# Letting layer 1 of a graph-network kernel begin inside the last pair of layer 0

## The chip, the cores and the metric

The kernel runs on one NeuronCore of a Trainium2 chip. The metric is the device time of one execution in microseconds (us). Its five engines have queues of their own and run side by side: TensorE (PE, matrix products), VectorE (DVE), ScalarE (ACT), GpSimd (POOL) and SyncE (SP, which here only issues DMA transfers). Each works through its queue strictly in order, and waits for the others by semaphores. The kernel before took 2484.26 us, the median of three runs (2483.71 to 2485.73).

## The reference

Two layers act on a batch of 64 matrices x of 256 x 256 (32 pairs of two), with one shared 256 x 256 matrix adj. All is float32.

```
# layer 0
h = max(layernorm(x), 0);  G = adj * adj
h = relu(G (h W1)); h = relu(G (h W2)); x = x + G (h W3)     # W1 256x512, W2 512x1024, W3 1024x256
# layer 1
h = max(layernorm(x), 0)
deg = adj.sum(0) + adj.sum(1) - diag(adj)
L = diag(deg)^-1/2 (diag(deg) - adj) diag(deg)^-1/2
U = eigenvectors of L (eigh)
x = x + U (relu((U^T h) V1 + b1) V2 + b2)                     # V1 256x128, V2 128x256
```

Layer 1 needs U, all the eigenvectors of a 256 x 256 symmetric matrix. They don't depend on x, so layer 0 can run while they are computed.

## The kernel before

**Two programs share the engines.** `Eigen.vectors` computes U and its transpose (tiles `u` and `ut`): a tridiagonal form, small eigenproblems of 16, and four levels of merging. It is a long chain of small steps, most on DVE. The class `Layers` does everything with x, pair by pair. Layer 0 of pair q is a sequence of PE products (`first`, `second`, `third`, `fourth`, `last`), each bank of results moved out of PSUM by ACT. `last` adds the result to x on DVE and gives x1. `norm1` then normalizes x1 for layer 1: eight ACT sums (`junk`), small DVE steps on 128 x 4 (`nm`, `v`, `tmp`, `s`, `scale`, `shift`), four ACT passes that write `h`. `turn_rows` transposes `h` on PE, with two ACT copies back, and `for_layer1` multiplies it by V1 (`L_gnn_W` against `h`) into the tile `hw`. In the program's products each instruction appears in the trace as two weight loads and two matmul rows (a transpose as one).

For pairs 0 to 29, x1 and hw are spilled to DRAM; those of the last two pairs (`KEPT = 2`) stay in SBUF.

**The order of the work on PE and ACT is written out by a planner.** The class `Pace` keeps a clock for each engine and estimated durations. The eigenvector program issues through `pace.now`, whose `chain` places an instruction at the time at which its inputs are ready; before it, `run` issues instructions of layer 0's two streams (`products`, for PE, and `rows`, for loading and normalizing) that can start earlier. `pace.finish()` issues what is left of the streams. So PE multiplies for layer 0 in the gaps of the eigenvector chain. DVE, POOL and SP keep their program order in this part or are ordered by the framework's scheduler.

**The hand-over to layer 1.** The last instructions of `vectors` are two products that ACT copies into `u` and `ut`, and a product that adds up counters of missed convergence over the partitions; DVE turns it into an integer `flag`. Then `pace.finish()` issues the rest of layer 0. After that `Eigen.mend` (L1690, L1691) has every engine load `flag` into a register and branch: with a flag over zero, a slower eigensolver is run. It is zero here, and every engine jumps over that body (about 70 PE and 15,000 DVE instructions). The framework's DVE order puts one `x <- x, bank` addition of the last pair ahead of the branch, the other behind it; the rest of the last pair's normalization, its transposes and its product with V1 stand behind it too.

**Layer 1** (`layer1`) takes the pairs in the order 30, 31, 0, 1, ..., 29. In step i it fetches the pair three steps ahead (`fetch`: hw of 256 KB and x1 of 512 KB by SP, L1971 and L1973), does `to_vectors` of pair i (PE `hw` against `u`, DVE `z`, ACT `s`, POOL `xb` = x1 + U b2), `from_vectors` of pair i-1 (PE `s` against `ut`, ACT `g`) and `finish` of pair i-2 (PE `g` against V2, DVE `out`, a store by SP). Its tiles lie in memory that the eigenvector program's pools gave back, so the first transfer waits until every engine is past the branch.

Of the kernel before, what the change touches and what calls it, by code (L numbers as in the profile page):

```python
# [27 lines left out]
N = 256  # L28
P = 128
H = 2  # L30
PAIRS = 32
KEPT = 2
LN_EPS = 1e-5
EPS = 2.0**-24
BIG = 1.0e3
# [108 lines left out]
class Pace:  # L144
# [6 lines left out]
    LATER = {"PE": 0.2, "ACT": 0.1}  # L151

    def __init__(self, nc):
        self.slower = self.SLOWER
        self.now = Proxy(nc, self.chain)
        self.later = Proxy(nc, lambda op: op)
        self.clock = dict.fromkeys(ENGINES.values(), 0.0)
        self.written, self.read, self.streams, self.on = {}, {}, [], True
# [32 lines left out]
    def chain(self, op):  # L191
        if not self.on:
            return op.call(*op.args, **op.kwargs)
        late = self.LATER.get(op.engine, 0.0)
        self.run(self.ready(op) + late, "ACT" if op.engine == "ACT" else None)
        return self.issue(op, self.slower)

    def run(self, limit, whole=None):
# [14 lines left out]
    def complete(self, stream):  # L213
        while stream.more:
            if stream.head() is not None:
                self.issue(stream.op)
                stream.op = None

    def finish(self):
        self.run(float("inf"))  # L220
# [1474 lines left out]
class Layers:  # L1695


    def __init__(self, tc, ctx, ap, gt2, u, ut):
        self.tc, self.nc, self.ap = tc, tc.nc, ap
        self.gt2, self.u, self.ut = gt2, u, ut  # L1700
        pool = ctx.enter_context(tc.tile_pool(name="layers", bufs=1))
        self.kept = ctx.enter_context(tc.tile_pool(name="kept", bufs=KEPT))
        dram = ctx.enter_context(tc.tile_pool(name="dram", bufs=1, space=bass.MemoryType.DRAM))
        self.x1, self.hw = {}, {}
        self.x, self.h0, self.y1, self.y2, self.s2, self.p3, self.h1, self.new = ({} for _ in range(8))
        self.begun = set()
        self.spilled = {
            q: dram.tile([P, H * 2 * N], F32, name=f"x1_{q}") for q in range(PAIRS - KEPT)
        }
        self.spilled_hw = {  # L1710
            q: dram.tile([P, H * 2 * P], F32, name=f"hw_{q}") for q in range(PAIRS - KEPT)
        }
        self.w = {}
        for name in ("L0_gnn_W1", "L0_gnn_W2", "L0_gnn_W3", "L1_gnn_W1", "L1_gnn_W2"):
            rows, cols = ap[name].shape
            self.w[name] = pool.tile([P, rows // P, cols], F32, name=name)
        self.b1 = pool.tile([P, P], F32, name="b1")
        self.eye = pool.tile([P, P], F32, name="eye")
        self.b2 = pool.tile([P, N], F32, name="b2")
        self.u1 = pool.tile([P, H], F32, name="u1")  # L1720
        self.ub2 = pool.tile([P, H, N], F32, name="ub2")
# [11 lines left out]
        for h in range(H):  # L1733
            yield self.nc.sync.dma_start(out=x[:, h], in_=self.view(self.ap["x"], q)[:, h])

    def open(self, ctx, name, io, work, banks):

        self.io = ctx.enter_context(self.tc.tile_pool(name=name + "_io", bufs=io))
        self.wp = ctx.enter_context(self.tc.tile_pool(name=name + "_work", bufs=work))
        self.sp = ctx.enter_context(self.tc.tile_pool(name=name + "_stat", bufs=2))  # L1740
        self.ps = ctx.enter_context(self.tc.tile_pool(name=name + "_psum", bufs=banks, space=PSUM))

    def view(self, t, q):
        return t[2 * q : 2 * q + 2].rearrange("b (h p) f -> p h b f", p=P)
# [3 lines left out]

    def group(self, out, pairs):
        for i, (lhsT, rhs) in enumerate(pairs):  # L1750
            self.nc.tensor.matmul(out, lhsT=lhsT, rhs=rhs, start=i == 0, stop=i == len(pairs) - 1)  # L1751

    def products_of(self, out, pairs):
        for i, (lhsT, rhs) in enumerate(pairs):
# [51 lines left out]
    def products(self):  # L1806


        yield lambda: 0 in self.h0
        yield from self.first(0)  # L1810
        yield from self.second(0)
        for q in range(PAIRS):
            more = q + 1 < PAIRS
            yield from self.third(q)
            if q > 0:
                yield lambda: q - 1 in self.h1
                yield from self.turn_rows(q - 1)
            yield from self.fourth(q, 0)
            if q > 0:
                yield from self.for_layer1(q - 1)  # L1820
            if more:
                yield lambda: q + 1 in self.h0
                yield from self.first(q + 1)
            yield from self.fourth(q, 1)
            if more:
                yield from self.second(q + 1)
            yield from self.last(q)
        yield lambda: PAIRS - 1 in self.h1
        yield from self.turn_rows(PAIRS - 1)
        yield from self.for_layer1(PAIRS - 1)  # L1830

# [127 lines left out]

    def turn(self):  # L1960

        nc = self.nc
        nc.vector.tensor_reduce(self.u1, self.u, AX.X, OP.add)  # L1963
        for h in range(H):
            nc.vector.tensor_scalar(self.ub2[:, h, :], self.b2, self.u1[:, h : h + 1], None, OP.mult)

    def fetch(self, q):
        x1, hw = self.x1.get(q), self.hw.get(q)
        if x1 is None:
            hw = self.io.tile([P, H, 2, P], F32, tag="hw", name="hw1")  # L1970
            self.nc.sync.dma_start(out=hw.rearrange("p h b k -> p (h b k)"), in_=self.spilled_hw[q])  # L1971
            x1 = self.io.tile([P, H, 2, N], F32, tag="x", name="x1")
            self.nc.sync.dma_start(out=x1.rearrange("p h b f -> p (h b f)"), in_=self.spilled[q])  # L1973
        return x1, hw

    def to_vectors(self, x1, hw):

        nc = self.nc
        z = self.wp.tile([P, H, 2, P], F32, tag="z", name="z")
        ps = self.bank()  # L1980
        for m in range(H):
            self.group(
                ps[:, m * N : (m + 1) * N],
                [
                    (self.u[:, h, m * P : (m + 1) * P], hw[:, h].rearrange("p b k -> p (b k)"))
                    for h in range(H)
                ],
            )
        nc.vector.tensor_tensor(
            z.rearrange("p h b k -> p (h b) k"),  # L1990
            ps.rearrange("p (g k) -> p g k", k=P),
            self.b1.unsqueeze(1).to_broadcast([P, H * 2, P]),
            OP.add,
        )
        s = self.wp.tile([P, H, 2, P], F32, tag="s", name="s")
        nc.scalar.activation(s, z, AF.Relu)
        xb = self.wp.tile([P, H, 2, N], F32, tag="xb", name="xb")
        for b in range(2):
            nc.gpsimd.tensor_tensor(xb[:, :, b, :], x1[:, :, b, :], self.ub2, OP.add)  # L1999
        return s, xb  # L2000

    def from_vectors(self, s):

        g = self.wp.tile([P, 2 * N], F32, tag="g", name="g")
        ps = self.bank()
        for b in range(2):
            self.group(
                ps[:, b * N : (b + 1) * N], [(s[:, m, b, :], self.ut[:, m, :]) for m in range(H)]
            )
        self.nc.scalar.copy(g, ps)  # L2010
        return g

    def finish(self, q, g, xb):
        nc = self.nc
        out = self.io.tile([P, H, 2, N], F32, tag="out", name="out")
        for m in range(H):
            ps = self.bank()
            for b in range(2):
                at = b * N + m * P
                self.group(  # L2020
# [2 lines left out]
            nc.vector.tensor_tensor(flat(out)[:, m, :], flat(xb)[:, m, :], ps, OP.add)  # L2023
            nc.sync.dma_start(out=self.view(self.ap["out"], q)[:, m], in_=out[:, m])

    def layer1(self):

        ahead = 3
        order = [*self.x1, *self.spilled]
        got = {i: self.fetch(order[i]) for i in range(KEPT + ahead)}  # L2030
        mid, tail = {}, {}
        with self.tc.manual_schedule():
            for i in range(PAIRS + 2):
                if KEPT + ahead <= i + ahead < PAIRS:
                    got[i + ahead] = self.fetch(order[i + ahead])
                if i < PAIRS:
                    mid[i] = self.to_vectors(*got.pop(i))
                if 0 <= i - 1 < PAIRS:
                    s, xb = mid.pop(i - 1)
                    tail[i - 1] = self.from_vectors(s), xb  # L2040
                if 0 <= i - 2:
                    self.finish(order[i - 2], *tail.pop(i - 2))
# [7 lines left out]
def tile_kernel(ctx: ExitStack, tc: tile.TileContext, ap):  # L2050
    pool = ctx.enter_context(tc.tile_pool(name="shared", bufs=1))
    gt2, u, ut = (pool.tile([P, H, N], F32, name=c) for c in ("gt2", "u", "ut"))
    layers = Layers(tc, ctx, ap, gt2, u, ut)
    with ExitStack() as inner:
        pace = Pace(tc.nc)
        eigen = Eigen(tc, inner, ap, gt2, pace)
        layers.open(inner, "l0", io=2, work=1, banks=4)

        layers.nc = pace.later
        for op in layers.load(0):  # L2060
# [2 lines left out]
        layers.load_weights()  # L2063
        eigen.load_rest()

        layers.nc = pace.later
        pace.streams = layers.streams()
        with tc.manual_schedule(engines={mybir.EngineType.PE, mybir.EngineType.Activation}):
            eigen.vectors(u, ut)
            pace.finish()  # L2070
        layers.nc = tc.nc
        eigen.mend(u, ut)
    layers.open(ctx, "l1", io=5, work=4, banks=8)
    layers.turn()
    layers.layer1()


INS = [
# [30 lines left out]
```

## Time and profile before

| | |
|---|---|
| median of the runs | 2484.26 us |
| the profiled execution | 2484.25 us, span on the core 2482.4 us |
| PE busy | 2401.1 us, 97% |
| DVE, ACT, POOL busy | 2152.8, 1009.6, 474.2 us |
| mean granted TensorE clock | 0.993 |
| DMA | 90.03 MB; mean share of the engines 0.75 to 0.80 in layer 1 |
| `flag` written | 2265.24 us into the span |
| first transfer of layer 1 | 2288.97 us |
| last matmul | 2477.9 us |

All positions in time below are microseconds from the start of the span. A row of the timeline gives the start and length of a run of like instructions, the engine, the line, the operation, the tiles as out<-in with shapes, the number of rows, and in brackets the idle time ahead of it and the engine and tile that ended it. Line 189 is the helper through which the planner issues everything; line 1751 is the helper of layer 1's products. PE is pipelined, so the length of a run includes the drain of its last matmul; from the start of one run to the start of the next is the better measure. In a row with windows of time, the figures behind the engines are the granted TensorE clock as a share of full speed, the DMA share, and GB/s.

### The profile page before, as it was taken

To read this page: it belongs to the slowest core of one execution; us is meant where nothing else is said; L and a number is where in the kernel's file an instruction comes from. 1 tells how busy PE (TensorE), PEld (TensorE's weight loads), DVE (VectorE), ACT (ScalarE), POOL (GpSimd) and SP (SyncE) were. 2 spreads that over 40 slices of the span, in tenths; PEclk is the share of its full clock that TensorE was granted. 3 is DMA by queue.
4 is the path that set the end of the run, shared out by engine and by line. 5 is a ranking of instruction groups with operands and counts; after the bars stand their busy time and mean duration, and the time that the engine had idled before them with its cause. 6 is when DMAs were issued, how large, how long until landed. Compare 5 with 4: busy or idle time off the path is not lost. (4 is left out here: it accounts for less than half of the span.)

```text
span 2482.4 us, 38245 instructions
## 1 busy us (share of the span) xinstructions
PE 2401.1 (97%) x8986; PEld 1551.4 (62%) x8986; DVE 2152.8 (87%) x13409; ACT 1009.6 (41%) x2826; POOL 474.2 (19%) x1625
## 2 busy tenths in 40 slices
PE   7999999999999999999999999999999999998899
PEld 4666655666565566656556666665566666665788
DVE  7999999999999999999999889998888887973333
ACT  4334444434444433344444244443444434343222
POOL 2333333334333111111110000000000000000343
PEclk9999999999999999999999999999999999999899
DMA  3000000000000000000000000000000000001476
GB/s 111 18 13 15 22 22 19 22 22 5 22 22 18 22 22 22 5 22 22 22 18 30 10 22 22 22 22 22 18 22 26 22 22 22 6 21 34 166 252 203
DMA packets 59401, 90.03 MB, mean 36 GB/s; under 512 B 5792, under 2 KB 42784, under 8 KB 59168
## 3 DMA queue, kind: packets, MB, share of 16 engines
q1 hardware_dynamic: 59168, 87.52, 10.7%
q8 instruction: 73, 1.20, 0.2%
q14 instruction: 160, 1.31, 0.2%
HBM read 47.13 MB, written 40.37 MB: 35 GB/s over the span
## 5 line engine op out<-in xcount | busy, mean ns | idle before, releaser
L189 PE MATMUL bank<-y,L_gnn_W 128*128 128x512 f32 x2048 | 905.5, 593 | 1.3 <-ACT y L189 1.3
L189 PEld LDWEIGHTS bank<-y,L_gnn_W 128*128 128x128 f32 x2048 | 379.3, 190 | 427.2 <-issue 410.9
L189 PE MATMUL bank<-L_gnn_W,s 128*128 128x256 f32 x2048 | 464.7, 381 | 2.2 <-ACT s L189 2.2
L189 PEld LDWEIGHTS bank<-L_gnn_W,s 128*128 128x128 f32 x2048 | 384.3, 191 | 51.8 <-ACT s L189 2.6
L189 ACT ACTIVATE s<-bank 128x512 f32<-128x512 f32 x384 | 224.3, 586 | 179.5 <-PE bank L189 178.2
L189 PE MATMUL bank<-gt,s 128*128 128x256 f32 x1024 | 230.3, 379 | 1.7 <-ACT s L189 1.7
L189 PE MATMUL bank<-L_gnn_W,y 128*128 128x512 f32 x512 | 228.8, 592 | 0.0
L189 PEld LDWEIGHTS bank<-gt,s 128*128 128x128 f32 x1024 | 192.1, 190 | 36.1 <-issue 9.6
L1999 POOL TENSOR_TENSOR xb<-x,ub 128x512 f32<-128x512 f32 x64 | 79.6, 1267 | 601.4 <-ACT junk L189 506.3
L189 ACT ACTIVATE s<-nn,guard 128x1 f32<-128x1 f32 x254 | 74.3, 293 | 252.2 <-DVE nn L189 235.7
L189 POOL COPY m<-xr 128x1 f32<-128x1 f32 x254 | 55.6, 219 | 548.1 <-DVE xr L189 535.7
L189 ACT ACTIVATE h<-x,shift,scale 128x256 f32<-128x256 f32 x256 | 135.9, 590 | 59.3 <-DVE shift L189 59.1
L189 ACT COPY y<-bank 128x512 f32<-128x512 f32 x192 | 110.8, 580 | 115.8 <-PE bank L189 114.8
L189 PEld LDWEIGHTS bank<-L_gnn_W,y 128*128 128x128 f32 x512 | 95.3, 190 | 97.8 <-issue 90.6
L189 ACT ACTIVATE junk<-xr 128x254 f32<-128x254 f32 (+63 forms) x127 | 45.9, 361 | 263.8 <-DVE xr L189 263.4
L189 ACT ACTIVATE junk<-x,nm 128x256 f32<-128x256 f32 x256 | 129.0, 504 | 26.8 <-DVE nm L189 22.2
L189 ACT ACTIVATE junk<-x 128x256 f32<-128x256 f32 x256 | 105.5, 412 | 83.1 <-DVE x L189 68.8
L189 DVE SCALAR_TENSOR_TENSOR A<-xr,wc,A 128x255 f32<-128x255 f32 (+63 forms) x381 | 139.3, 367 | 0.0
L189 DVE SCALAR_TENSOR_TENSOR A<-wr,q,A 128x255 f32<-128x255 f32 (+63 forms) x381 | 138.6, 365 | 0.0
L189 PEld LDWEIGHTS psB<-ident,ac 128*128 128x128 f32 x381 | 44.8, 135 | 148.1 <-PE bank L189 76.6
L189 DVE SCALAR_TENSOR_TENSOR q<-q 128x1 f32<-128x1 f32 (+1 forms) x576 | 119.4, 208 | 16.4 <-ACT q L189 5.6
L189 PE MATMUL bank<-gt,h 128*128 128x256 f32 x512 | 120.5, 386 | 0.4 <-ACT h L189 0.4
(604 smaller groups left out, 4375.4 us busy)
## 6 DMA issues: line engine op xcount, KB each, us to landing
x<-x SPq DMA_DIRECT2D x60, 512.0 KB, 3.6
x<-in_x_dram SPq DMA_DIRECT2D x64, 256.0 KB, 3.7
out_dram<-out SPq DMA_DIRECT2D x64, 256.0 KB, 2.2
hw<-hw SPq DMA_DIRECT2D x60, 256.0 KB, 2.6
L_gnn_W<-in_L_gnn_W_dram SPq DMA_DIRECT2D x1, 2048.0 KB, 11.0
L_gnn_W<-in_L_gnn_W_dram SPq DMA_DIRECT2D x1, 1024.0 KB, 13.6
L_gnn_W<-in_L_gnn_W_dram SPq DMA_DIRECT2D x1, 512.0 KB, 6.4
mask<-in_c_blk_dram SPq DMA_DIRECT2D x2, 256.0 KB, 2.6
```

Source lines behind the costliest of these rows:

```text
L189: return op.call(*op.args, **op.kwargs)
L1999: nc.gpsimd.tensor_tensor(xb[:, :, b, :], x1[:, :, b, :], self.ub2, OP.add)
```

## The change

- The planner's streams are no longer emptied ahead of the branch. Behind the flag product, 6 us of PE work by the planner's clock (`FLAG_US`) are issued (`pace.go_on`), then the branch on all engines.
- Layer 1 is now issued through the planner (`pace.now`, with `no_haste`: an instruction of layer 1 is placed one step behind its engine's clock, and stream instructions that are ready go in front). So products of layer 1 alternate with what is left of layer 0's last pair on PE.
- Layer 1's order becomes 0 to 10, 30, 31, 11 to 29. The stream's last part (transposes of pair 31 and its product with V1) is held back by `self.due` until step 8, then issued whole.
- `turn` (DVE: row sums of U and U b2) becomes the first thing behind the branch, in layer 1's written order.
- Layer 1 has pools of its own (`open1`) while layer 0's stay open: five buffers for fetched tiles, three instead of five for `out`, four for its work tiles, and PSUM banks taken in turn from a new pool of four and layer 0's pool of four (before: one pool of eight).

The PE queue of the changed kernel, as its built program has it (x counts program instructions): nine of the sixteen products of `fourth(31, 0)`, the flag's load and the branch, one more of them, then

```
hw(0),u x4 in turn with fourth(31,0) x6 | hw(1),u x4 in turn with for_layer1(30) x8
ut,s(0) x4 and hw(2),u x4 and ut,s(1) x4 in turn with fourth(31,1) x16
last(31) x4 in turn with V2,g(0) x4
hw(3) x4, ut,s(2) x4, V2,g(1) x4, ... five such steps, up to hw(7), ut,s(6), V2,g(5)
transposes of h(31) x8, for_layer1(31) x8, then hw(8) x4 ... to the end as before
```

Behind the branch, SP first issues hw and x1 of pairs 0, 1, 2, 3, 4, then of 5 as pair 0's are freed. DVE's order there is: `turn`, z(0), z(1), z(2), x(31) first half, out(0) first half, x(31) second half, out(0) second half, nm, z(3), out(1) first half, v, out(1) second half, tmp, tmp, s, s, scale, shift, z(4), out(2), ... ACT's is: s(0), p(31), s(1), hw(30), g(0), s(2), p(31), g(1), six of the eight sums of pair 31, s(3), a sum, g(2), a sum, the root, two of four `h`, s(4), `h`, g(3), `h`, s(5), g(4), ...

```diff
@@ -30,6 +30,8 @@
 H = 2
 PAIRS = 32
 KEPT = 2
+LAST_AT = 12
+FLAG_US = 6.0
 LN_EPS = 1e-5
 EPS = 2.0**-24
 BIG = 1.0e3
...
@@ -191,8 +193,10 @@
     def chain(self, op):
         if not self.on:
             return op.call(*op.args, **op.kwargs)
-        late = self.LATER.get(op.engine, 0.0)
-        self.run(self.ready(op) + late, "ACT" if op.engine == "ACT" else None)
+        due = self.ready(op) + self.LATER.get(op.engine, 0.0)
+        if self.no_haste:
+            due = max(due, self.clock[op.engine] + 0.01)
+        self.run(due, "ACT" if op.engine == "ACT" and not self.no_haste else None)
         return self.issue(op, self.slower)
 
     def run(self, limit, whole=None):
@@ -215,6 +219,9 @@
             if stream.head() is not None:
                 self.issue(stream.op)
                 stream.op = None
+
+    def go_on(self, us):
+        self.run(self.clock["PE"] + us)
 
     def finish(self):
         self.run(float("inf"))
...
@@ -1733,12 +1741,25 @@
         for h in range(H):
             yield self.nc.sync.dma_start(out=x[:, h], in_=self.view(self.ap["x"], q)[:, h])
 
-    def open(self, ctx, name, io, work, banks):
-
-        self.io = ctx.enter_context(self.tc.tile_pool(name=name + "_io", bufs=io))
-        self.wp = ctx.enter_context(self.tc.tile_pool(name=name + "_work", bufs=work))
-        self.sp = ctx.enter_context(self.tc.tile_pool(name=name + "_stat", bufs=2))
-        self.ps = ctx.enter_context(self.tc.tile_pool(name=name + "_psum", bufs=banks, space=PSUM))
+    def open(self, ctx):
+
+        self.io = ctx.enter_context(self.tc.tile_pool(name="l0_io", bufs=2))
+        self.wp = ctx.enter_context(self.tc.tile_pool(name="l0_work", bufs=1))
+        self.sp = ctx.enter_context(self.tc.tile_pool(name="l0_stat", bufs=2))
+        self.ps = ctx.enter_context(self.tc.tile_pool(name="l0_psum", bufs=4, space=PSUM))
+
+    def open1(self, ctx):
+
+        self.io1 = ctx.enter_context(self.tc.tile_pool(name="l1_io", bufs=5))
+        self.op = ctx.enter_context(self.tc.tile_pool(name="l1_out", bufs=3))
+        self.wp1 = ctx.enter_context(self.tc.tile_pool(name="l1_work", bufs=4))
+        self.ps1 = ctx.enter_context(self.tc.tile_pool(name="l1_psum", bufs=4, space=PSUM))
+        self.turns = 0
+
+    def bank1(self):
+
+        self.turns += 1
+        return (self.ps1 if self.turns % 2 else self.ps).tile([P, 512], F32, tag="bank", name="bank")
 
     def view(self, t, q):
         return t[2 * q : 2 * q + 2].rearrange("b (h p) f -> p h b f", p=P)
...
@@ -1825,7 +1846,7 @@
             if more:
                 yield from self.second(q + 1)
             yield from self.last(q)
-        yield lambda: PAIRS - 1 in self.h1
+        yield lambda: PAIRS - 1 in self.h1 and self.due
         yield from self.turn_rows(PAIRS - 1)
         yield from self.for_layer1(PAIRS - 1)
 
...
@@ -1967,17 +1988,17 @@
     def fetch(self, q):
         x1, hw = self.x1.get(q), self.hw.get(q)
         if x1 is None:
-            hw = self.io.tile([P, H, 2, P], F32, tag="hw", name="hw1")
-            self.nc.sync.dma_start(out=hw.rearrange("p h b k -> p (h b k)"), in_=self.spilled_hw[q])
-            x1 = self.io.tile([P, H, 2, N], F32, tag="x", name="x1")
-            self.nc.sync.dma_start(out=x1.rearrange("p h b f -> p (h b f)"), in_=self.spilled[q])
+            hw = self.io1.tile([P, H, 2, P], F32, tag="hw", name="hw1")
+            self.now.sync.dma_start(out=hw.rearrange("p h b k -> p (h b k)"), in_=self.spilled_hw[q])
+            x1 = self.io1.tile([P, H, 2, N], F32, tag="x", name="x1")
+            self.now.sync.dma_start(out=x1.rearrange("p h b f -> p (h b f)"), in_=self.spilled[q])
         return x1, hw
 
     def to_vectors(self, x1, hw):
 
-        nc = self.nc
-        z = self.wp.tile([P, H, 2, P], F32, tag="z", name="z")
-        ps = self.bank()
+        nc = self.now
+        z = self.wp1.tile([P, H, 2, P], F32, tag="z", name="z")
+        ps = self.bank1()
         for m in range(H):
             self.group(
                 ps[:, m * N : (m + 1) * N],
...
@@ -2023,15 +2044,21 @@
             nc.vector.tensor_tensor(flat(out)[:, m, :], flat(xb)[:, m, :], ps, OP.add)
             nc.sync.dma_start(out=self.view(self.ap["out"], q)[:, m], in_=out[:, m])
 
-    def layer1(self):
+    def layer1(self, pace):
+
 
         ahead = 3
-        order = [*self.x1, *self.spilled]
-        got = {i: self.fetch(order[i]) for i in range(KEPT + ahead)}
+        last = PAIRS - 1
+        order = [*range(LAST_AT - 1), last - 1, last, *range(LAST_AT - 1, last - 1)]
+        got = {i: self.fetch(order[i]) for i in range(ahead)}
         mid, tail = {}, {}
         with self.tc.manual_schedule():
+            self.turn()
             for i in range(PAIRS + 2):
-                if KEPT + ahead <= i + ahead < PAIRS:
+                if i == LAST_AT - 1 - ahead:
+                    self.due = True
+                    pace.finish()
+                if i + ahead < PAIRS:
                     got[i + ahead] = self.fetch(order[i + ahead])
                 if i < PAIRS:
                     mid[i] = self.to_vectors(*got.pop(i))
@@ -2051,10 +2078,10 @@
     pool = ctx.enter_context(tc.tile_pool(name="shared", bufs=1))
     gt2, u, ut = (pool.tile([P, H, N], F32, name=c) for c in ("gt2", "u", "ut"))
     layers = Layers(tc, ctx, ap, gt2, u, ut)
+    layers.open(ctx)
+    pace = Pace(tc.nc)
     with ExitStack() as inner:
-        pace = Pace(tc.nc)
         eigen = Eigen(tc, inner, ap, gt2, pace)
-        layers.open(inner, "l0", io=2, work=1, banks=4)
 
         layers.nc = pace.later
         for op in layers.load(0):
@@ -2063,16 +2090,16 @@
         layers.load_weights()
         eigen.load_rest()
 
-        layers.nc = pace.later
+        layers.nc, layers.now = pace.later, pace.now
         pace.streams = layers.streams()
         with tc.manual_schedule(engines={mybir.EngineType.PE, mybir.EngineType.Activation}):
             eigen.vectors(u, ut)
-            pace.finish()
-        layers.nc = tc.nc
+            pace.go_on(FLAG_US)
+        pace.on = False
         eigen.mend(u, ut)
-    layers.open(ctx, "l1", io=5, work=4, banks=8)
-    layers.turn()
-    layers.layer1()
+    pace.on, pace.no_haste, pace.slower = True, True, 1.0
+    layers.open1(ctx)
+    layers.layer1(pace)
 
 
 INS = [
```

## The prediction

> **What bounds the kernel now.** First the page's busy times and its 40 slices (62 us each).
>
> ```profile
> PE 2401.1 (97%) x8986; PEld 1551.4 (62%) x8986; DVE 2152.8 (87%) x13409; ACT 1009.6 (41%) x2826; POOL 474.2 (19%) x1625
> PE   7999999999999999999999999999999999998899
> PEclk9999999999999999999999999999999999999899
> ```
>
> TensorE bounds nearly everything. Only the first and the 37th and 38th slices fall below 9, and in the 38th the granted clock falls too. The change can therefore win only the hole around 2290 us. PE's own timeline shows that hole.
>
> ```profile
> 2283.42 3.25 PE L189 MATMUL bank<-p,gt 128*128 128x512 f32 x7
> 2301.48 0.47 PE L189 MATMUL bank<-eye,h 128*128 128x128 f32 x1 [14.80 <-ACT h L189]
> 2302.47 1.82 PE L189 MATMUL bank<-eye,h 128*128 128x128 f32 x7 [0.51 <-ACT h L189]
> 2304.80 3.85 PE L189 MATMUL bank<-L_gnn_W,h 128*128 128x128 f32 x16 [0.52 <-ACT h L189]
> 2309.32 6.24 PE L1751 MATMUL bank<-hw,u 128*128 128x256 f32 x16 [0.67 <-ACT hw L189]
> 2315.40 1.89 PE L1751 MATMUL bank<-ut,s 128*128 128x256 f32 x8
> ```
>
> PE ends pair 31's `last` at 2286.67, stands 14.80 us for that pair's `h`, and runs what follows at half speed: 16 rows of `hw,u` take 6.1 us to the next start, where eight like rows of `ut,s` later take 1.73 (2315.40 to 2317.13). What fills the hole is read from the chain that ended last.
>
> ```profile
> 2289.47 0.69 DVE x L189
> ...
> 2300.83 1.59 ACT h L189 x3
> ...
> 2309.32 168.56 PE bank L1751 x768
> ```
>
> It runs through pair 31's addition, normalization, transposes and V1 product, and from 2309.32 through products alone. From there the kernel is bound by PE at 5.18 us a pair, with DMA at 0.8. Last, what the branch costs: SP's waits around the hand-over, and the first row of DVE behind the branch.
>
> ```profile
> SPq L1971 <- PEq L1690: 17.9, 1, 17.9
> SPq L1971 <- ACTq L1690: 2.4, 1, 2.4
> SPq L1971 <- DVEq L1691: 2.0, 1, 2.0
> ```
>
> ```profile
> 2288.86 0.69 DVE L1963 TENSOR_REDUCE u<-u 128x2 f32<-128x512 f32 x1 [3.18 <-DVEq L1691]
> ```
>
> SP's first transfer (2288.97) waits for every engine: 17.9 us for PE, then 2.4 for ACT, 2.0 for DVE. Counted back, PE's load of the flag passed at 2288.97 - 2.0 - 2.4 = 2284.6, two microseconds ahead of PE's last matmul.
>
> **The change, step by step.** *What is removed: the hole.* From 2286.67 to 2315.40 are 28.73 us. The work in it at full speed is eight transposes 0.87 (pair 30's: 2266.52 to the next start 2267.39), the V1 product 1.79 (pair 30's: 2274.30 to 2276.09) and 16 rows of `hw,u` 3.46 (twice 1.73), in all 6.12. So 22.6 us are lost now. All this work stays, and so does the sum of the products: the same number for each pair, and layer 1 ends with the same steps. The order ahead of the branch is unchanged on PE, so both kernels agree up to there.
>
> *The branch inside PE's stream.* PE reaches it behind nine of `fourth(31, 0)`'s sixteen products: 2267.39 + 18 rows x 0.216 (32 rows take 2267.39 to 2274.30) = 2271.3. The flag is there at 2265.24, and ACT's last instruction ahead of its branch ends at 2268.55; PE is the last. How long PE stands, no row shows: before, it waited for `h` anyway. Above: DVE's 3.18 us. The Trainium skill speaks against the move too (Runtime: NRT & Kernel Launch, Instruction fetch mechanics): a taken branch to a target outside the fetched window stalls on a fetch. But it gives PE room for 2048 instructions, and PE's skipped body has some 70[...]. I take 1.0, nearer the low end, because PE's flag load passed two microseconds early, hidden behind queued products. The clean-up of layer 0's last additions, no longer ahead of DVE's branch, costs nothing: DVE then stands at the branch from 2265 on.
>
> *The first fetch.* Behind SP's wait are queued the ten transfers of pairs 0 to 4, and all later ones; PE's second product behind the branch waits for the first. Before, layer 1 began with pairs kept in SBUF and hid this. SP issues 0.1 after PE's passing, and hw lands 2.6 us later by the page's row:
>
> ```profile
> hw<-hw SPq DMA_DIRECT2D x60, 256.0 KB, 2.6
> ```
>
> So hw(0) is there at 2271.3 + 1.0 + 0.1 + 2.6 = 2275.0. One product of 0.43 lies in between: PE is idle 3.7 - 0.4 = 3.3 us. With branch 0.1 and landing 2.0 it is 1.8; with 3.2 and 3.0, 5.9. Pair 0's x1 is wanted by POOL only, whose `xb` is used some 25 us later. The second hw is behind 1 MB in the queue, wanted some 4 us after the first, with about 3 us to spare; `turn` (1.3 us of DVE) runs within PE's hole.
>
> *The clock.* Does a hole of 3.7 us with 0.4 us of work inside halve the clock? PE's timeline has two earlier gaps, and windows of half a microsecond show the clock around the second.
>
> ```profile
> 1720.33 1.91 PE L189 MATMUL bank<-L_gnn_W,s 128*128 128x256 f32 x4 [2.20 <-ACT s L189]
> ...
> 1786.46 1.24 PE L189 MATMUL psB<-ident,m 128*128 128x128 f32 x4 [3.47 <-DVE m L189]
> ```
>
> ```profile
> 1785.00:1785.50 0.50, 0.00 (x0) 0.00 (x0) 0.50 (x7) 0.00 (x0) 0.00 (x0) 0.90 0.00 0
> ...
> 1792.00:1792.50 0.50, 0.50 (x3) 0.33 (x3) 0.00 (x0) 0.00 (x0) 0.00 (x0) 0.78 0.00 0
> ```
>
> The clock (third figure from the end) fell at 1785.4, 2.4 us into an idle time of 3.47, and came back at 1792.2: 5.8 us of PE at half speed, 2.9 lost. At 2309.32 to about 2314.5 it was 5.1 us and 2.6. A gap of 2.20 (1720) did not lower it. The Trainium skill (TensorE: Matmul & The Clock Gate, Part 1) asks for a whole idle window of 3.4 us, counted by a free-running clock. By the page 0 here, since the product cuts the hole; by the row, which fell with a third of such a window busy, 2.7 in about half of the positions of the window. I follow the row: 1.3 (0 to 3.4).
>
> *Mixed products.* Products of both layers in turn cost no more than apart: each loads its own weights either way. ACT's copies and DVE's z come between them with room: s(0) is ready some 3 us ahead of ut,s(0). The banks are eight as before. A gain is excluded too, since PE has no gaps there now.
>
> *Pair 31's normalization, moved into layer 1's queues.* Eight sums, a root, four `h` (7 us of ACT), seven small DVE steps, two additions. It is wanted five pairs (25.9 us) after the start of hw(3) and is ready at about 15: those products hide it. A price can come from what is queued behind it: z(4) stands behind `shift`. Counting from the start of hw(3): the sums end at 6.1, POOL's `xb(5)` (7.05 to 9.55) collides with the steps as before, where `s` and `shift` took 1.0 to 1.2 us instead of 0.2; shift at 10.2, z(4) 10.9, s(4) behind two `h` at 11.9; PE wants it at 12.1. I take 0.3 (0 to 3). Without that cover it would be the old 15 us again.
>
> *Transposes of pair 31* stand directly ahead of the V1 product, which waits for two ACT copies: about 0.9 (before, 0.52 stood in the same place, half hidden by half speed).
>
> Sum: 22.6 - 3.3 - 1.3 - 0.9 - 0.3 = 16.8. The profiled execution took 2484.25 (span 2482.4 and 1.85 around it), the same as the median of the runs: 2484.25 - 16.8 = **2467.5 us**.
>
> **The rivals.** *A dearer hand-over* (2470 to 2475): DVE's 3.18 us holds for PE, the landing is late, the clock falls, and z(4) and z(5) come late: 5.9 + 2.9 + 0.9 + 3 = 12.7 lost, 2474.3. For it, the row of 3.18 and the tight margin of 0.2; against it, that they must come together.
>
> *No gain* (2480 to 2487): the hole moves instead of closing. The fetch needs all engines past the branch; a longer one there, say 12 us, with a cold clock eats the rest. For it speaks SP's 17.9 us; against it, these were waited for PE's own work, which is now left behind.
>
> *Slower*: three `out` buffers instead of five. The place is DVE's `out(i)`, which waits for the store of pair i-3. A buffer may be held 3 x 5.18 = 15.5 us; today 1.5 for DVE, 1.2 for issues and 2.2 to land make 5. To lose the 16.8 and 5 more, each of 31 pairs must take 0.7 longer, so a store must take over 12 us. DMA at 0.8 says not.
>
> That the change doesn't do what it says is excluded for the order: the built queues show it.
>
> **How the numbers follow.** The main case has 0.82, the dearer hand-over 0.13, no gain 0.03, slower 0.02. The main case alone runs from 22.6 - 2.7 = 19.9 (2464.4) to about 12 (2472). The range that leaves out at most 2 in 10 takes in most of the dearer hand-over: 2463.5 to 2473.5. A measurement of this kernel tells 0.2% (5 us) from no change: faster 0.95, same 0.03, slower 0.02.
>
> **What the changed profile would show.** PE's first product on hw 3 to 4 us behind the branch, with a wait for a transfer; no row of idle over 5 us after 2260; the granted clock at 1.00 or low for one stretch of 3 to 6 us; the transposes about 55 us behind the branch, with no wait for `h`; pairs at 5.18 us. Wrong would make it: a fetch issued long after PE's passing, a PE branch of many microseconds, or pairs above 5.2 us.

## The result and the profile after

The changed kernel took 2468.23 us, the median of four runs (2467.95 to 2469.64); the kernel before, run beside it, 2484.99 us (2483.71 to 2485.79). The ratio is 0.9934, with a 95% interval of 0.9917 to 0.9951. The forecast was 2467.5, with a range of 2463.5 to 2473.5. The profiled execution took 2468.13 us, its span 2466.3.

Executions of the common part, up to the flag, differ by up to a few us from run to run (the flag is there between 2263.7 and 2266.4 us in the traces below). A difference that leaves this out is the distance from the end of the row that writes `flag` to the end of PE's last row. Before it is 212.64 us (2265.24 to 2477.88), after it 196.63 (2265.62 to 2462.25): 16.0 us less. The sum on record was 16.8.

First the busy times and two slice rows of the page of the changed kernel:

```profile
PE 2396.4 (97%) x8986; PEld 1546.4 (63%) x8986; DVE 2151.9 (87%) x13409; ACT 1011.8 (41%) x2826; POOL 476.8 (19%) x1625
PE   7999999999999999999999999999999999999999
PEclk9999999999999999999999999999999999999999
```

PE's two slices of 8 near the end are gone, and so is the one of its clock. The numbers of instructions are the same on all five engines, as the order had said: nothing but waiting was removed. (Line 191 is now the planner's helper, 195 the helper behind its end, and 1697 and 1698 are the lines of the load of the flag and of the branch; in the experiments with `HOLD_US` all of them are one higher.) PE's timeline has two waits left behind the flag:

```profile
2267.77 4.87 PE L191 MATMUL bank<-L_gnn_W,s 128*128 128x256 f32 x20
2276.03 1.19 PE L191 MATMUL bank<-hw,u 128*128 128x256 f32 x2 [3.39 <-DMA hw<-hw]
...
2279.52 0.60 PE L191 MATMUL bank<-hw,u 128*128 128x256 f32 x2
...
2328.77 1.04 PE L191 MATMUL bank<-eye,h 128*128 128x128 f32 x8
2330.43 2.32 PE L191 MATMUL bank<-L_gnn_W,h 128*128 128x128 f32 x16 [0.62 <-ACT h L191]
2332.58 1.89 PE L195 MATMUL bank<-hw,u 128*128 128x256 f32 x8
```

The first row holds the nine products ahead of the branch and the one behind it, and the branch does not part it (PE is idle 0.15 us in the window from 2268 to 2272). Its 20 rows are 4.32 us of work at 0.216 each, but the next row starts 8.26 us after it: 3.94 us are lost, 0.15 of them at the branch and the rest for hw(0). From 2276.03 to 2279.52 eight rows take 3.49 us instead of 1.73: 1.76 are lost to the clock. The transposes of pair 31 and its V1 product take 3.81 us up to the next row instead of 0.87 + 1.79: 1.15 are lost to ACT's copies. Together 6.85 of the old 22.6 remain, and 15.75 of the 16.0 gained are accounted for; the other 0.25 is found below.

The chain that ended last (start, length, what) reads the same:

```profile
2272.05 3.01 DMA hw<-hw
2275.07 0.97 issue
2276.03 53.67 PE bank L191 x243
...
2329.79 0.60 ACT h L191
2330.38 0.04 issue
2330.43 2.32 PE bank L191 x16
2332.74 129.52 PE bank L195 x600
```

Neither `x` nor the sums or the small DVE steps of pair 31's normalization are in it any more. What is left of the hand-over is one transfer, and 0.97 us behind it that no row explains.

### The profile page after: what moved, and what is told of

It reads as the page before. It is cut to its first block, busy times and chain, and to the rows that moved or that the text cites. A ratio compares the mean times of both kernels' runs of the same rounds, so it can differ in the third digit from the quotient of the medians.

```text
span 2466.3 us, 38232 instructions
## 1 busy us (share of the span) xinstructions
PE 2396.4 (97%) x8986; PEld 1546.4 (63%) x8986; DVE 2151.9 (87%) x13409; ACT 1011.8 (41%) x2826; POOL 476.8 (19%) x1625
## 5 line engine op out<-in xcount | busy, mean ns | idle before, releaser
L191 POOL TENSOR_TENSOR xb<-x,ub 128x512 f32<-128x512 f32 x16 | 19.9, 1271 | 516.0 <-DMA hw<-hw 491.5
## 6 DMA issues: line engine op xcount, KB each, us to landing
L_gnn_W<-in_L_gnn_W_dram SPq DMA_DIRECT2D x1, 2048.0 KB, 10.2
```

## The experiments

All times are medians; "flag to end" is the distance described above, in the profiled execution. Kernels with the same time of before ran on one chip beside it. The changed kernel took 2467.66 us when it was run again (flag to end 196.99), and the experiments are compared with that.

| | us | before, beside it | ratio | flag to end |
|---|---|---|---|---|
| changed kernel, again | 2467.66 | 2483.82 | 0.9934 | 196.99 |
| 6 us of layer 0 held behind the branch | 2463.04 | 2483.82 | 0.9915 | 191.84 |
| the same, transposes one step earlier | 2462.52 | 2483.82 | 0.9912 | 191.06 |
| last pairs as 8th and 9th | 2477.7 (one run) | 2483.82 | | 205.59 |
| no product ahead of the branch | 2472.35 | 2484.09 | 0.9952 | 200.80 |
| before, without the branch | 2479.51 | 2484.09 | 0.9982 | 208.66 |
| changed, without the branch | 2460.64 | 2484.09 | 0.9905 | 190.92 |
| the new order, nothing interleaved | 2480.73 | 2484.09 | 0.9985 | 208.54 |
| held, transposes earlier, V1 product later | 2461.64 | 2481.89 | 0.9916 | 190.17 |
| last pairs as 10th and 11th | 2467.82 | 2481.89 | 0.9942 | 197.30 |

**Is the hole that is left the fetch, and does the half clock follow from it?** Layer 0's products are kept for the time in which hw(0) is on its way.

```diff
+HOLD_US = 6.0
...
             self.turn()
+            pace.go_on(HOLD_US)
             for i in range(PAIRS + 2):
```

> Behind the branch, 6 us of what is left of layer 0's products are issued ahead of layer 1's first product. My theory (the hand-over's rest): in the changed kernel PE stood 3.9 us for the first transfer and then ran 3.4 us at half clock (1.7 lost). Both go: 2468.1 - 3.9 - 1.7 = 2462.5 (2461.5 to 2464), no idle row of PE over 1 us at hw,u, granted clock 1.00 throughout. Rival A (the microsecond between the landing, 2275.07, and PE's start, 2276.03, is PE working through the long list of waits of that instruction, whenever it comes): about 1 us of idle stays ahead of the first hw,u, 2463.5. Rival B (the half clock comes from the branch, not from the idle time): the clock still falls, 2464.2.

It took 2463.04 us (2462.7 to 2463.91; ratio 0.9915, 0.9898 to 0.9931), 4.6 less than the changed kernel. From PE's timeline:

```profile
2272.13 3.26 PE L192 MATMUL bank<-L_gnn_W,s 128*128 128x256 f32 x14 [0.73 <-PEq L1699]
2275.22 1.95 PE L192 MATMUL bank<-L_gnn_W,h 128*128 128x128 f32 x16
2277.01 1.89 PE L192 MATMUL bank<-L_gnn_W,s 128*128 128x256 f32 x8
2278.74 0.59 PE L192 MATMUL bank<-hw,u 128*128 128x256 f32 x2
```

`hw,u` now has no bracket: it waits for nothing. The granted clock is 1.00 in every window from 2268 to 2338, so without the hole there is no half speed, and the two losses are one cause. The 0.97 us between landing and start does not show either, which fells the rival as it was put (a wait that comes whenever the instruction comes). A price that is paid beside the products queued ahead is not excluded by this. PE stood 0.73 at the branch, against 0.39 in the changed kernel's second execution; that is a part of what the gain fell short of the full 5.7.

**Does the last wait, of the V1 product for ACT's copies, go when the transposes come earlier?**

```diff
-                if i == LAST_AT - 1 - ahead:
+                if i == LAST_AT - 2 - ahead:
                     self.due = True
+                if i == LAST_AT - 1 - ahead:
                     pace.finish()
```

> As e1, and pair 31's transposes are given free one step earlier than the rest, so that products of layer 1 stand between the transposes, the two copies by ACT and the product with V1. My theory: the 0.8 us ahead of that product and 0.36 us inside it were waits for the two copies; they go: 1.1 us below e1, 2461.4. Rival (the row is slow by itself, or the wait moves to the next product): the same as e1.

2462.52 us (2461.6 to 2463.76), not to be told from the first experiment by the medians. PE's timeline says why:

```profile
2320.71 0.60 PE L192 MATMUL bank<-eye,h 128*128 128x128 f32 x4
2321.93 0.49 PE L192 MATMUL bank<-L_gnn_W,h 128*128 128x128 f32 x2 [0.62 <-ACT h L192]
```

The planner put the V1 product straight behind the last transposes again, so the wait of 0.62 stayed. A miss, of the edit and not of the reading: the product itself has to be held. The last of the experiments does so.

**Do the five pairs hide the normalization, and how many are needed?** `LAST_AT = 8` in place of 12: the last pairs are taken as 8th and 9th instead of 12th and 13th.

> The last pairs come as 8th and 9th of layer 1 instead of 12th and 13th, so pair 31's transposes stand one step (5.2 us) behind the start of hw(3) instead of five (25.9). My theory (the gain is the cover: pair 31's normalization hidden by layer 1's products): h was written 12.6 us after the start of hw(3), so PE stands about 7 us at the transposes, and runs after it for 3.4 to 6 us at half clock (2.6 lost): 2468.1 + 9.5 = 2477.5 (2475 to 2480). Rival (the gain comes from the branch's place or from the new pools, the normalization would be fast with PE waiting): 2468 to 2470.

2477.7 us, one run. From PE's timeline:

```profile
2314.31 0.33 PE L191 MATMUL bank<-eye,h 128*128 128x128 f32 x1 [4.77 <-ACT h L191]
2315.29 1.82 PE L191 MATMUL bank<-eye,h 128*128 128x128 f32 x7 [0.65 <-ACT h L191]
2317.63 3.84 PE L191 MATMUL bank<-L_gnn_W,h 128*128 128x128 f32 x16 [0.52 <-ACT h L191]
```

With one pair in place of five between hw(3) (2304.19) and the transposes, the old waits for `h` are back, and the half clock with them: the V1 product takes 3.6 us to the next start. 8.6 us of the gain return (205.59 against 196.99).

**And at 10?** The last pairs come as 10th and 11th (the expectation counts these places from 0).

> Edit: the last pairs are taken as 9th and 10th of layer 1 instead of 11th and 12th, so that pair 31's transposes come two steps (10.4 us) earlier. In the changed kernel its h was written 12.6 us after hw(3) had started, and the transposes were called 25.9 us after it; here they are called 15.5 us after it. My theory: what counts is only whether h is there; 2.9 us are left over, so the time is that of the changed kernel, 2467.7 within 0.5 us, and no PE wait for h ahead of the transposes. Rival: the order of ACT and DVE around the end of the normalization is the limit and the cover was needed in full, so PE waits 1 to 5 us for h: 2469 to 2473.

2467.82 us (2466.86 and 2468.77), on another chip than the changed kernel. By flag to end it is 197.30, against 196.63 and 196.99: the same, but for a first transfer that took 3.43 us instead of 3.01 and 3.22. The transposes have no wait, and the V1 product has its usual one:

```profile
2317.16 1.04 PE L191 MATMUL bank<-eye,h 128*128 128x128 f32 x8
2318.82 2.32 PE L191 MATMUL bank<-L_gnn_W,h 128*128 128x128 f32 x16 [0.62 <-ACT h L191]
```

So three pairs (15.5 us) are cover enough, one (5.2) is not; two were not tried. This agrees with `h`, whose last row in the changed kernel ends 12.6 us after the start of hw(3) (2302.87 to 2315.44). The 12th and 13th place leave two pairs to spare.

**Is PE's branch cheap only because its load of the flag is hidden behind queued products?** `FLAG_US = 0.0` in place of 6.0.

> Edit: no product of layer 0 is issued between the flag product and the branch, so PE comes to its load of the flag as the flag is being written (about 2265 us) and nearly all of fourth(31, 0) lies behind the branch. My theory: PE's branch cost only 0.15 to 0.4 us in the changed kernel because the load of the flag was over before the queued products ended; here it is exposed, so PE stands 2 to 4 us at the branch, as DVE does. The fetch then leaves SP when the last engine (DVE or PE) is past, about 2269.5, lands at 2272.5, and finds fewer than ten products to cover it only in part: more of fourth(31, 0) is left behind the branch and is issued in turn with hw(0), which waits. In all 3 to 5 us more than the changed kernel: 2470.5 to 2473. Rival: PE's branch is nearly free wherever it stands, and the time is that of the changed kernel, 2467.7 within 1 us.

2472.35 us (2471.66 to 2473.46; ratio 0.9952, 0.9933 to 0.9972), 4.7 more than the changed kernel: the forecast time, but not for the forecast reason. From PE's timeline:

```profile
2266.27 1.10 PE L191 MATMUL bank<-y,L_gnn_W 128*128 128x512 f32 x2 [0.59 <-PEq L1698]
2273.45 1.19 PE L191 MATMUL bank<-hw,u 128*128 128x256 f32 x2 [6.09 <-DMA x<-x]
```

PE comes to the flag as it is written (2265.10) and still stands only 0.59 us. The part of my theory that gave PE 2 to 4 us falls; the rival was right on PE's branch and wrong on the time. What costs is the fetch: SP's longest wait for a branch in that stretch is now 3.0 us, for DVE, whose first row behind it starts at 2269.57 after 4.46 us of standing there. PE has one product left for the 7 us to hw(0). It then runs at half speed for 5.5 us (0.50 in the windows from 2272 to 2278, 0.75 in that from 2278 to 2280), so 2.8 are lost, against 1.76.

**How much of the old hole was the branch itself?** The kernel before, without the slower solver for missed cases, the load of the flag and the branch:

```diff
-        eigen.mend(u, ut)
```

> The kernel before without the branch: the slower eigensolver for missed cases, and the load of the flag and the jump over it on every engine, are left out. It tells what part of the hole of 22.6 us the branch itself made. My theory: without it the second addition of pair 31 comes 2.6 us earlier, POOL's U b2 products run before the small DVE steps of the last normalization instead of beside them (those steps then take 0.2 us instead of 1.0 to 1.2, about 5 us in all), and the chain addition, sums, root, h, transposes, V1 product stays: about 7.6 us less, 2476.2, the hole still over 8 us. Rival A: the branch delays only the addition, 2.6 us, 2481.2. Rival B: the branch is the cause of the hole, and without it the time is that of the changed kernel or below, 2463 to 2468.

2479.51 us (ratio 0.9982, 0.9974 to 0.999): 4.6 less than before, not 7.6. From PE's timeline, and then DVE's:

```profile
2281.84 3.68 PE L189 MATMUL bank<-p,gt 128*128 128x512 f32 x8
2296.98 0.48 PE L189 MATMUL bank<-eye,h 128*128 128x128 f32 x1 [11.46 <-ACT h L189]
```

```profile
2292.66 1.19 DVE L189 TENSOR_TENSOR s<-s,tmp 128x4 f32<-128x4 f32 x1
```

The hole shrinks by 3.34 us (14.80 to 11.46): 2.8 by the second addition, which no longer stands behind the branch, and nearly all of the rest by `nm`, which takes 0.33 us instead of 0.95. Another 0.6 of the 4.0 us by flag to end comes behind the hole, where the half clock ends earlier (16 rows of `hw,u` take 5.35 us instead of 6.08). That POOL would be through before the small steps was wrong: its additions wait for `x` of the last pair, whichever way, and start at 2286.47, so `s` takes 1.19 us as before. So 11.46 of the 14.80 us that PE stood were the last pair's additions and normalization with nothing beside them.

**What does the branch cost the changed kernel?** The same line left out there.

> The changed kernel with the same part left out (no slower eigensolver, no load of the flag, no branch). My theory: the first fetch then waits for no engine to pass a branch but only for the memory of the eigenvector pools, goes out at about 2266 and lands while PE has products queued; the idle time of 3.5 to 3.9 us ahead of hw,u, the 3.4 us at half clock (1.7) and the branch's 0.2 to 0.4 go: 5.7 less than the changed kernel, 2462. Rival: the fetch still waits for an engine's last use of that memory that comes late, and a part of the hole stays: 2465 to 2467.5.

2460.64 us (2460.2 and 2461.07; ratio 0.9905, 0.9876 to 0.9933), 7.0 less than the changed kernel, 6.1 by flag to end. The timeline has no wait at all from the flag to the V1 product:

```profile
2266.61 4.48 PE L191 MATMUL bank<-L_gnn_W,s 128*128 128x256 f32 x20
2270.93 0.59 PE L191 MATMUL bank<-hw,u 128*128 128x256 f32 x2
```

The 3.94 + 1.76 us are thus the price of the branch, nearly all of it through the fetch behind it. The rest of the 6.1 is of the size of the spread between two executions of the changed kernel (196.63 and 196.99).

**Or do the order of the pairs and the pools bring the gain?** The changed kernel with layer 0 issued whole ahead of the branch:

```diff
-            pace.go_on(FLAG_US)
+            layers.due = True
+            pace.finish()
...
-                if i == LAST_AT - 1 - ahead:
-                    self.due = True
-                    pace.finish()
```

> The changed kernel's order of pairs, pools and transfers, but layer 0 is issued whole ahead of the branch, with its transposes and the V1 product of pair 31, as the streams were emptied before: no product of layer 0 is left to lie between the products of layer 1. My theory: the gain comes from overlapping, not from the order 0 to 10, 30, 31 or the pools, so the hole of the kernel before comes back ahead of the transposes (PE waits for h, which waits for the additions and the normalization), and the branch and the fetch lie behind it in PE's order: at least as slow as before, 2484 to 2490. Rival: the order and the pools bring most of the gain, 2468 to 2472.

2480.73 us (ratio 0.9985, 0.9978 to 0.9992), 3.4 us below before, 13.1 above the changed kernel. PE's timeline:

```profile
2284.16 3.68 PE L191 MATMUL bank<-p,gt 128*128 128x512 f32 x8
2293.68 3.75 PE L191 MATMUL bank<-hw,u 128*128 128x256 f32 x8 [5.83 <-ACT junk L191]
2302.95 0.47 PE L191 MATMUL bank<-eye,h 128*128 128x128 f32 x1 [5.53 <-ACT h L191]
```

The hole is there again, in two pieces. hw(0) now lies inside it, ahead of the transposes in PE's queue, and fills 3.5 us of it, at half clock; my bound "at least as slow as before" missed this. The planner had issued the transposes by then, so it was not the planner that put hw(0) ahead of them; what did is not on record. The order and the pools together are worth some 4 us (208.54 against 212.64), and the interleaving the other 12.

**And when the V1 product is held as well?** The second experiment, with the V1 product held one step longer by a condition of its own:

```diff
         yield from self.turn_rows(PAIRS - 1)
+        yield lambda: self.due1
         yield from self.for_layer1(PAIRS - 1)
...
                 if i == LAST_AT - 2 - ahead:
                     self.due = True
                 if i == LAST_AT - 1 - ahead:
+                    self.due1 = True
                     pace.finish()
```

> Edit to the version that holds 6 us of layer 0 behind the branch (first experiment): pair 31's transposes are let go one step of layer 1 earlier, and its V1 product is held until that step's other products (ut,s and V2,g, 3.46 us) are behind it in PE's order. In the second experiment the V1 product still stood straight behind the transposes and waited 0.62 us for ACT's copy. My theory: ACT's two copies are long done when the V1 product starts, so the wait and the longer start go, 0.9 to 1.15 us less than the first experiment's 2463.0: 2462.0, no PE wait over 0.3 us behind hw(0). Rival: the copies are placed in ACT's order behind other work and PE waits for them in another place, 2463.0.

2461.64 us (2460.3 to 2462.81; ratio 0.9916, 0.9899 to 0.9932). This ran on another chip than the first experiment (before took 2481.89 there), and by the ratio the two can't be told apart (0.9916 and 0.9915). What changed is read from one execution of each, by flag to end: 190.17 against 191.84. PE's timeline:

```profile
2320.87 0.60 PE L192 MATMUL bank<-eye,h 128*128 128x128 f32 x4
2321.30 1.89 PE L192 MATMUL bank<-ut,s 128*128 128x256 f32 x8
2323.03 1.89 PE L192 MATMUL bank<-L_gnn_W,g 128*128 128x256 f32 x8
2324.76 1.95 PE L192 MATMUL bank<-L_gnn_W,h 128*128 128x128 f32 x16
2326.55 1.89 PE L196 MATMUL bank<-hw,u 128*128 128x256 f32 x8
```

The V1 product has no bracket, and takes 1.79 us to the next start. Its wait is gone (1.1), and about 0.6 more came from the branch, where PE's windows of this execution show 0.15 us idle and the first experiment's row 0.73. The second part is the branch's own spread and no merit of the edit: the second experiment shows no wait at the branch either. Its flag to end is as short as that of the changed kernel without any branch (190.92, with the V1 wait still in it). PE's timeline shows no wait of more than 0.2 us behind the flag.

## Why the prediction was right

**The hole.** The waits of 22.6 us were to go, and they went. The sum was short by 0.2: it counts from 2286.67, the end of `last`'s row, which includes the drain. Its eight rows of 0.43 us end at 2286.43, and from there 22.85 us were lost; less the 6.85 that remain this is the measured 16.0. That overlapping removes the hole, and neither the new order with its pools nor the branch alone, is shown by the two kernels that do only one of these (4.1 and 4.0 us by flag to end).

**The branch in PE's stream** was taken at 1.0 us, well under DVE's row of 3.18. It is 0.15 (PE's idle time in the window from 2268 to 2272), and 0.39, 0.40, 0.59, 0.65 and 0.73 in five of the experiments. The page of the Trainium skill that the prediction names (Runtime: NRT & Kernel Launch, Instruction fetch mechanics) was the better guide than DVE's row, as PE's body fits the room that it states; a time for such a branch it does not give. My argument for the low end was a flag load that passes early behind queued products. It isn't needed: PE stood only 0.59 with the load exposed. Whether the queue hides something in the changed kernel stays open. The branch has a record of its own (length in ns, start in us), first in the changed kernel, then with no product ahead:

```profile
L1698 PEldq COMPARE_BRANCH  x1: 3347/3347/3347, 2268.4 to 2268.4; - x1
```

```profile
L1698 PEldq COMPARE_BRANCH  x1: 369/369/369, 2265.7 to 2265.7; - x1
```

The long one ends about where the queued products end (2271.7). It can be waiting for them, or they can be hiding it; in the kernel before it took 0.375 us with 2 us of products queued. DVE stood 3.91 in the changed kernel:

```profile
2269.54 0.69 DVE L191 TENSOR_REDUCE u<-u 128x2 f32<-128x512 f32 x1 [3.91 <-DVEq L1698]
```

It was past 2.4 us before PE, so it cost nothing there. With PE early, DVE is the one that SP waits for.

**The first fetch** was taken to be there 2.7 us after PE's passing, and to leave PE idle for 3.3 us. PE's passing did set the issue; SP waited for it last, 2.4 us beyond DVE's (us in total, times, longest):

```profile
SPq L191 <- PEq L1698: 2.4, 1, 2.4
```

The issue took 0.2 us instead of 0.1 and the transfer 3.01 instead of 2.6, and PE began 0.97 after that, a time that the prediction put at nothing: 1.5 us more than taken. That the idle time is 3.94 us, only 0.6 more than taken, is luck: the branch, 0.85 smaller than taken, makes up for more than half. Even so this is the term of the sum that was most mis-sized, and it hung on reading "landing" as "start of the consumer".

**The clock** was taken at 1.3, half of the 2.7 of a fall, because a product cuts the hole. The windows of half a microsecond (the clock is the third figure from the end) show that it fell:

```profile
2276.00:2276.50 0.50, 0.47 (x1) 0.50 (x2) 0.00 (x0) 0.00 (x0) 0.00 (x0) 0.53 0.93 369
...
2279.00:2279.50 0.50, 0.50 (x2) 0.40 (x2) 0.00 (x0) 0.00 (x0) 0.50 (x1) 0.55 1.08 426
```

It was low from 2276.03 to 2279.45, some 3.4 us, and cost 1.76. It fell in all four executions with such a hole (the two of the changed kernel, and those with the last pairs at 8 and at 10).

Two readings of the prediction were wrong here. The product does not cut the hole in the middle: it runs right behind the branch, and PE then stands 3.39 us or more at a stretch. And the gap of 2.20 us at 1720 did lower the clock. The prediction's own row shows it (four rows of 256 columns in 1.91 us, where eight take 1.89 elsewhere), and so do windows of 3.41 us, here of the kernel before (the two around 1720.5) and of the kernel with no product ahead of the branch (the last):

```profile
1717.13:1720.54 3.41, 1.21 (x6) 0.76 (x5) 3.34 (x38) 0.96 (x3) 0.00 (x0) 1.00 0.00 0
1720.54:1723.96 3.42, 3.42 (x9) 2.71 (x9) 2.98 (x19) 0.83 (x3) 0.00 (x0) 0.50 0.00 0
```

```profile
2265.34:2268.75 3.41, 1.44 (x3) 0.30 (x2) 0.00 (x0) 0.60 (x1) 0.00 (x0) 1.00 0.04 12
```

What the traces show is a grid. In all twelve the low stretches last 3.41 us or a multiple of it (3.41 at 2276.03, 6.8 at 1785.4, 10.2 in the kernel with no product ahead, 23.9 in the old hole), and when a trace is laid out in stretches of 3.41 us from one fall, all its changes lie on the borders. The clock fell 28 times, after stretches with PE busy for 0.00 to 1.57 us (the first figure behind the length; 1.21 and 1.44 above). Behind the first 60 us of the traces it never fell after a stretch with more, and it stayed up only once with less than 1.56, after one with 1.47. So the free-running window of the page (TensorE: Matmul & The Clock Gate, Part 1) agrees with the traces, but the window doesn't have to be wholly idle: a little under half busy still lets the clock fall. By this a hole of 3.4 to 3.8 us lets the clock fall in most positions of the grid, and 3.4 us at half clock cost 1.7 (an estimate from these figures). The 1.3 came near by luck: it is an even chance of 2.7, where the traces have four falls of four at 1.7 to 1.8.

**Pair 31's normalization in layer 1's queues** was to cost 0.3 and cost nothing. The collision came as forecast, as DVE's timeline shows:

```profile
2309.56 1.12 DVE L191 TENSOR_TENSOR s<-s,tmp 128x4 f32<-128x4 f32 x1
2310.71 1.20 DVE L191 TENSOR_SCALAR s<-s 128x4 f32<-128x4 f32 x1
2311.94 0.18 DVE L191 RECIPROCAL scale<-s 128x4 f32<-128x4 f32 x1
```

But `v`, `tmp` and `shift` fell outside POOL's rows (2309.37 to 2311.88) and took 0.16 to 0.17. s(4) ended at 2313.97, and PE wanted it at 2314.95. `h` was ready 12.6 us after the start of hw(3), not at about 15. **The transposes and the V1 product** cost 1.15 instead of 0.9. **Mixed products** cost nothing: a pair takes 5.18 us as before.

In sum: the hole 22.85 instead of 22.6, idle time 3.94 instead of 3.3, clock 1.76 instead of 1.3, the V1 wait 1.15 instead of 0.9, the queues 0 instead of 0.3. The misses make 0.8 us, the gain 16.0 instead of 16.8. The mechanism was right but for the clock's rule and the time between landing and start; that the sum is as close as this owes something to errors that cancel. Of the rivals, the dearer hand-over came true in its landing (3.0) and in that the clock fell, but not in its branch or its queues. A fetch of some 12 us, or a store that holds up the `out` buffers, was not seen.

## What to carry to other kernels

When a phase ends in a chain of small steps on other engines, let the next phase's big products start inside it: what counted here is how far apart the chain's start and its consumer lie, and one look at the chain's length (12.6 us here) says how many units of work to put between (three of 5.18 were enough, one was not). Where the new phase begins with a transfer that can't be issued earlier, keep back enough of the old phase's ready work to cover issue, landing and the start after it; here 6 us more of it were worth 4.6 us, because the short stall also halves the clock for 3.4 us behind it. Ask of a branch which engine passes last, since that one releases the transfers, and not what it costs the busiest engine.

## What the runs showed of the hardware

- The same branch, over a body that is never run, held PE for 0.15 to 0.73 us and DVE for 3.11 to 4.46 us. PE's price was 0.59 with its load of the flag exposed. The record of PE's branch is 0.37 us long in three of the traces and 3.35 to 4.01 in seven, the latter where it came with some 3.3 us of products queued. What sets the value within the 0.15 to 0.73, and whether those products hide a part, stays open.
- Where PE was already waiting for hw(0), its product began 0.97, 0.88, 0.97 and 0.97 us after the recorded landing of that tile (the changed kernel twice, and with the last pairs at 8 and at 10). Where the tile had landed earlier, no such time shows. Whether it is the record of the landing, the signal's way or the instruction's waits, taken up only after the landing, was not tried.
- The granted clock changed on a grid of 3.41 us. It fell after a stretch of the grid in which PE was busy for less than some 1.5 us (28 falls in twelve traces, after 0.00 to 1.57), and stayed low for 3.41 us or a multiple. In the kernel before, a gap of 2.20 us was enough.
- DVE's steps on 128 x 4 took 1.1 to 1.2 us instead of 0.2 while POOL ran its 128 x 512 additions, in the kernel before, without its branch, and in the changed kernel alike. Not every step is hit: `RECIPROCAL` took 0.18 us beside POOL's rows too (2296.20 in the kernel before). No run took POOL's rows away, so that they are the cause is inferred from the times alone.
